# The exact pieces of the normalised tokens of a second attention, in two tiles, one for each half of the tokens

## The chip, the cores and the metric

The kernel runs on one core of a Trainium2 chip. Its time is the time of one execution on the device in microseconds (us); shown is the median of three runs. TensorE (PE) multiplies matrices, VectorE (DVE), ScalarE (ACT) and GpSimd (POOL) work on elements, and SyncE (SP) starts transfers (DMA).

## The reference

1024 tokens of 512 channels pass through four blocks with a residual sum each: attention A (32 heads of 16 channels in 8 groups), a mixture of 8 experts of rank 16 on top of a base layer, attention B (32 heads of 128 channels, 8 groups of keys and values, weights of 4 bits with a scale for each 128 input channels, rotary positions, causal), and the same mixture of experts again.

```python
def _dequant_matmul(x, qw, scales):
    w = (qw.astype(jnp.float32) - ZERO) * jnp.repeat(scales, GS, axis=0)
    return x @ w
...
x = x + _L0_attn_a_ref(_layernorm(x, axis=-1), ...)
x = x + _L0_ffn_ref(_layernorm(x, axis=-1), ...)
x = x + _L0_attn_b_ref(_layernorm(x, axis=-1), ...)   # q, k, v and output by _dequant_matmul
x = x + _L0_ffn_ref(_layernorm(x, axis=-1), ...)
```

## The kernel before

The tokens stay on the chip in x_sb, in four blocks `a` of 256 tokens (two halves of 128 rows each). The sequence is attention A (to about 480 us), the first experts (to about 550), attention B head by head (to about 1380), and the second experts.

For attention B the normalised tokens are kept turned (channels on the 128 partitions) and in two pieces that sum to the number exactly: a high one in the format that TensorE takes at full rate, and a low one with the rest. Both lie in one tile, x_hl, of 128 partitions x 2 pieces x 4 chunks of channels x 1024 tokens. They are made by `halves_of_x(a, xn)`, once for each block: `norm.turned` transposes the eight 128x128 squares of the block on TensorE (line 185) into two PSUM banks, two chunks in each; for each bank ScalarE copies the high piece (line 755) and VectorE subtracts it for the low piece (line 756). The rows `xn` come from `ready(a)`: statistics (lines 149 and 150 on VectorE), root on ScalarE (154), reciprocal and shift on VectorE (155, 156), and then the rows by VectorE (162) and ScalarE (170). The statistics of a block need its sum with the experts' output (line 670, VectorE).

They are read by `scaled`, which makes one half (512 tokens) of a head's query, key or value: for each of four chunks `exact` multiplies the whole-number weights with the high piece (line 798) and the low piece (799) into one PSUM bank, and the result is scaled and summed, the first chunk by ScalarE (line 810), the others by VectorE (812). PSUM has five banks (`ac_ps`) for all of this. Queries and keys are then rotated: a transfer through SyncE's queue (822, 823) swaps halves of the partitions and lines 824 to 826 multiply and add, on GpSimd, for the first query on VectorE.

The order of TensorE's instructions is the order of the program text (`tc.manual_schedule`). Around the change it is: halves_of_x of blocks 0 and 1 between parts of the experts; keys(0) and queries(0) on the first half of the tokens; the last experts' matmuls; halves_of_x(2); values(0) on the first half (the matmuls of all four chunks); halves_of_x(3); then the first head's scores with the second halves of keys(0) and queries(0), woven in by two lists of due work (`short`, `long`). The order on VectorE, ScalarE, GpSimd and SyncE is made when the kernel is built, by a planner that takes the program's order as priority and its own estimate of times. The same library adds all waits between engines, from what each instruction reads and writes of a tile.

In the last head `reload(i, total)` brings the experts' weights back from DRAM in seven parts into the room of x_hl (lines 1087 and 1088); the second experts read them there.

Of the kernel before, what the change touches and what calls it, by code (L numbers as in the profile page):

```python
# [11 lines left out]
F32 = mybir.dt.float32  # L12
F32R = mybir.dt.float32r
# [3 lines left out]
ALU = mybir.AluOpType  # L17
# [3 lines left out]
P = 128  # L21
S = 1024
C = 512
NC_ = C // P
# [17 lines left out]
def kernel(  # L42
# [28 lines left out]
    nc = tc.nc  # L71

    def pool(stack, name, bufs=1, space=None):
        kw = {} if space is None else {"space": space}
        return stack.enter_context(tc.tile_pool(name=name, bufs=bufs, **kw))
# [28 lines left out]
    order = const.tile([P, 1, E], F32, name="order")  # L104
# [10 lines left out]
    def place_ffn_weights(room):  # L115
        at = 0
        for name, n, width in ("base", NC_, C), ("ar", NC_, AR), ("b", 1, C), ("bias", 1, C):
            fw[name] = room[:, at : at + n * width].rearrange("p (c o) -> p c o", o=width)
            at += n * width
        return room[:, :at]  # L120
# [17 lines left out]
    class Norm:  # L138
# [13 lines left out]
        def scale(self, a0, a1):  # L152
            some = slice(2 * a0, 2 * a1)
            nc.scalar.activation(self.rstd[:, some], self.mv[:, some, 1], AF.Sqrt, bias=eps_t)
            nc.vector.reciprocal(self.rstd[:, some], self.rstd[:, some])
            nc.vector.scalar_tensor_tensor(
                self.shift[:, some], self.mv[:, some, 0], -1.0, self.rstd[:, some], ALU.mult, ALU.mult
            )
# [16 lines left out]
                scale=self.rstd[:, t + 1 : t + 2],  # L175
            )

        def turned(self, a, xn, bank, natural, store):

            for cp in range(NC_ // 2):  # L180
                tp = bank()
                by = tp.rearrange("q (c h p) -> q c h p", c=2, h=2)
                for c in range(2):
                    for h in range(2):
                        nc.tensor.transpose(by[:, c, h, :], xn[:, h, ts(2 * cp + c, P)], ident)  # L185
                order = "q c (p h) -> q c h p" if natural else "q c (h p) -> q c h p"
                store(
                    lambda dst: dst[:, 2 * cp : 2 * cp + 2, ts(a, 2 * P)].rearrange(order, h=2), by
                )

    def to_xT(place, tp):
# [2 lines left out]
    norm = Norm()  # L194
# [478 lines left out]
    def attention_b():  # L673
# [5 lines left out]
        with ExitStack() as ph:  # L679
            one = pool(ph, "b_one")  # L680
# [2 lines left out]
            ac_ps = pool(ph, "b_ac_ps", 5, PSUM)  # L683

            v_sb = one.tile([P, NT, G * DB], F32, name="v_sb")
            x_hl = one.tile([P, 2, NC_, S], F32R, name="x_hl")
            cos_sb = one.tile([P, S], F32, name="cos_sb")
            sin_sb = one.tile([P, S], F32, name="sin_sb")
            yT = shared.rearrange("p (c s) -> p c s", c=NC_)
# [61 lines left out]

            def halves_of_x(a, xn):
                def store(place, tp):
                    high = place(x_hl[:, 0])
                    nc.scalar.copy(high, tp)
                    nc.vector.tensor_tensor(place(x_hl[:, 1]), tp, high.bitcast(F32), ALU.subtract)  # L756

                norm.turned(a, xn, bank, True, store)

# [35 lines left out]
            def exact(ps, lhsT, high, low):  # L797
                nc.tensor.matmul(ps, lhsT, high, start=True, stop=False)  # L798
                nc.tensor.matmul(ps, lhsT, low, start=False, stop=True)  # L799
# [2 lines left out]

            def scaled(acc, w, scale, half):

                tok = ts(half, C)
                for c in range(NC_):
                    pp = ac_ps.tile([P, C], F32, tag="acc", name="pp")
                    exact(pp, w[:, c], x_hl[:, 0, c, tok], x_hl[:, 1, c, tok])
                    if c == 0:
                        nc.scalar.activation(acc, pp, AF.Copy, scale=scale(c))  # L810
                    else:
                        nc.vector.scalar_tensor_tensor(acc, pp, scale(c), acc, ALU.mult, ALU.add)  # L812
                    yield 2 * FAST

            def rotated(dst, w, scale, engines=(nc.gpsimd, nc.gpsimd)):

                for half, eng in enumerate(engines):
                    tok = ts(half, C)
                    acc = work.tile([P, C], F32, tag="acc", name="acc")
                    yield from scaled(acc, w, scale, half)  # L820
                    turned = work.tile([P, C], F32, tag="turned", name="turned")
                    nc.sync.dma_start(turned[0:64], acc[64:128])
                    nc.sync.dma_start(turned[64:128], acc[0:64])
                    eng.tensor_tensor(dst[:, tok], acc, cos_sb[:, tok], ALU.mult)  # L824
                    eng.tensor_tensor(turned, turned, sin_sb[:, tok], ALU.mult)
                    eng.tensor_tensor(dst[:, tok], dst[:, tok], turned, ALU.add)  # L826
                    yield 0
# [10 lines left out]
            def values(g):  # L838

                vT = one.tile([P, S], F32, tag="vT", name=f"vT_{g}")  # L840
                w = wvs.pop(g)
                for half in range(2):
                    acc = work.tile([P, C], F32, tag="acc", name="acc")
                    yield from scaled(acc, w, lambda c: v_sc[:, c, g : g + 1], half)

                    nc.scalar.copy(
                        vT[:, ts(half, C)].rearrange("d (k r j) -> d k j r", j=4, r=32),
                        acc.rearrange("d (k j r) -> d k j r", j=4, r=32),
                    )
                    yield 0  # L850
                waiting.append([len(issued) + 2, [("v", g), 4 * FAST, turned_values(g, vT)]])
# [9 lines left out]
            def probabilities(n, t):  # L861

                qT, kT = qTs[n], kTs[n // J]
                keys = (t + 1) * P
                wide = t >= NT // 2 or (n == 0 and t == 1)
                sc = sc_ps.tile([P, S if wide else C], F32, tag=f"sc{wide}", name="sc")
                for k0 in range(0, keys, C):
                    k1 = min(k0 + C, keys)
                    nc.tensor.matmul(sc[:, k0:k1], qT[:, ts(t, P)], kT[:, k0:k1], start=True, stop=True)  # L869
                at = len(issued) - NT * (HEADS - 1)  # L870
                slot = LAST[at] if at >= 0 else SLOTS[len(issued) % 3]
                p = x_sb[:, slot].rearrange("p h c -> p (h c)")
                issued.append(t)
                p = p[:, :keys]

                m = work.tile([P, 1], F32, tag="m", name="m", bufs=3)
                nc.vector.tensor_tensor_reduce(  # L877
                    p, sc[:, :keys], causal[:, S - keys :], -1.0, BIG, ALU.add, ALU.min, m
                )
                total = work.tile([P, 1], F32, tag="total", name="total", bufs=3)  # L880
                nc.scalar.activation(p, p, AF.Exp, bias=m, scale=-1.0, accum_out=total)  # L881
                return p, total
# [5 lines left out]
            flat = xT.rearrange("p c o -> p (c o)")  # L888

            def placed(n, t, p):  # L890
# [37 lines left out]
            place = {  # L928
                0: flat[:, :384],
                2: flat[:, 384:1792],  # L930
                3: flat[:, 1792:3712],
                1: one.tile([P, 896], F32, name="pT_1"),
            }
            place = {k: v.rearrange("p (i x) -> p i x", i=4) for k, v in place.items()}
# [68 lines left out]
            with tc.manual_schedule(engines={mybir.EngineType.PE}):  # L1003
                with ExitStack() as fs:
# [34 lines left out]
                    moe.base(4)  # L1039
                    moe.finish(3)  # L1040
                    halves_of_x(0, xns[0])
                    ready(1)
                    moe.base(5)
                    moe.finish(4)
                    moe.base(6)
                    moe.finish(5)
                    halves_of_x(1, xns[1])
                    ready(2)
                    short += [[("k", 0), 16 * FAST, keys(0)], [("q", 0), 16 * FAST, queries(0)]]
# [5 lines left out]
                    moe.finish(7)  # L1055
                    ready(3)
                    halves_of_x(2, xns[0])
                    short.append([("v", 0), 16 * FAST, values(0)])
                    for _ in range(4):
# [20 lines left out]

                def reload(i, total):

                    flat = x_hl.rearrange("p i c s -> p (i c s)")
                    room = place_ffn_weights(flat.bitcast(F32))
                    width = -(-room.shape[1] // (NT - 1))
                    part = slice(i * width, min((i + 1) * width, room.shape[1]))
                    nc.vector.tensor_copy(flat[:, part.start : part.start + 1], total)
                    nc.sync.dma_start(room[:, part], w_kept[:, part])
# [9 lines left out]
                for n in range(HEADS):  # L1098
# [16 lines left out]
                    for i, t in enumerate(TURNS if n else [0, 1, 2, 4, 3, 5, 6, 7]):  # L1115
# [5 lines left out]
                        p, total = probabilities(n, t)  # L1121
# [163 lines left out]
```

## Time and profile before

| | us |
|---|---|
| median of three runs | 1445.62 (1443.53 to 1448.45) |
| the profiled execution | 1443.47 |
| its span, first to last instruction | 1441.6 |
| TensorE busy in the span | 1387.7 (96%) |
| VectorE, ScalarE, GpSimd busy | 1188.9, 868.2, 596.9 |
| lines 798 and 799 reading x_hl, 384 matmuls each | 183.5 and 153.0 |

| stretch, us | TensorE busy | VectorE busy | ScalarE busy | TensorE clock granted |
|---|---|---|---|---|
| 500 to 530 | 29.21 | 14.42 | 6.86 | 1.00 |
| 530 to 550 | 16.77 | 15.88 | 7.77 | 0.83 |
| 550 to 600 | 44.60 | 39.77 | 29.82 | 0.93 |
| 600 to 1300 | 690.30 | 629.35 | 474.40 | 1.00 |

Busy times are of one profiled execution. Matmuls overlap in their pipeline, so a busy TensorE is not one at its peak. An idle time in the timeline is put down to what ended it; a wait for several things is put down to the last.

### The profile page before, as it was taken

What the parts mean: (1) busy time and instruction counts of PE and PEld (TensorE: products, weight loads), DVE (VectorE), ACT (ScalarE), POOL (GpSimd) and SP (SyncE); (2) the same over time, 40 slices, a digit from 0 to 9 for tenths busy, and PEclk for the clock granted to TensorE, in tenths of its full rate; (3) what the DMA queues carried; (4) which work ended last, traced back from release to release, by engine and by line L of the source; (5) the groups of instructions that cost most, each with busy time, mean ns of one, the idle gap of its engine ahead of it and who ended that gap; (6) DMA issues with size and microseconds to landing.
All of it is one profiled execution on the core that took longest, in us unless ns stands there. A gap on an engine that the chain in (4) does not pass through costs nothing. (4 is left out here: it accounts for less than half of the span.)

```text
span 1441.6 us, 21145 instructions
## 1 busy us (share of the span) xinstructions
PE 1387.7 (96%) x6711; PEld 882.1 (61%) x6711; DVE 1188.9 (82%) x2491; ACT 868.2 (60%) x1642; POOL 596.9 (41%) x505
## 2 busy tenths in 40 slices
PE   6999999999999998899999999999999999999888
PEld 4444444444444545677677777777777777777664
DVE  4799979979893658789898998999998998989774
ACT  2166757757677325676576676676666676666630
POOL 4200000000000616566666767657667566645230
PEclk9999999999999998999999999999999999999999
DMA  4352423324240213655566565655655655565711
GB/s 126 61 100 48 69 42 56 62 35 70 48 134 2 86 66 98 153 138 148 140 147 156 126 149 145 149 143 140 149 140 145 145 137 141 139 137 119 193 57 59
DMA packets 113183, 158.47 MB, mean 110 GB/s; under 512 B 35008, under 2 KB 86912, under 8 KB 112944
## 3 DMA queue, kind: packets, MB, share of 16 engines
q1 hardware_dynamic: 106252, 135.51, 40.3%
q0 software_dynamic: 6752, 21.57, 5.6%
q8 instruction: 54, 0.88, 0.2%
q14 instruction: 57, 0.47, 0.1%
q10 hardware_dynamic: 68, 0.03, 0.0%
HBM read 33.03 MB, written 6.05 MB: 27 GB/s over the span
## 5 line engine op out<-in xcount | busy, mean ns | idle before, releaser
L387 ACT ACTIVATE pT<-st 128x512 f32<-128x512 f32 x512 | 264.6, 603 | 128.7 <-PE st L383 109.6
L343 DVE TENSOR_REDUCE m<-sc 128x1 f32<-128x512 f32 x512 | 319.8, 682 | 25.8 <-PE st L375 19.8
L869 PE MATMUL sc<-kT,qT 128*128 128x512 f32 (+3 forms) x768 | 292.0, 489 | 2.4 <-POOL qT L826 1.3
L881 ACT ACTIVATE x_sb<-x_sb,m 128x768 f32<-128x768 f32 (+7 forms) x256 | 197.0, 769 | 120.4 <-DVE m L877 117.7
L949 PE MATMUL pc<-xT,v_sb 128*128 128x256 f32 (+1 forms) x1024 | 240.4, 361 | 14.2 <-DMA xT<-blocks 14.0
L886 ACT ACTIVATE x_sb<-x_sb,total 128x768 f32<-128x768 f32 (+7 forms) x256 | 195.5, 771 | 70.4 <-DVE total L885 69.0
L949 PEld LDWEIGHTS pc<-xT,v_sb 128*128 128x128 f32 x1024 | 190.7, 189 | 49.5 <-issue 17.2
L877 DVE CUSTOM_DVE_ANT_0 x_sb<-sc,causal 128x768 f32<-128x768 f32 (+7 forms) x256 | 191.4, 748 | 27.5 <-PE sc L869 26.1
L334 PE MATMUL sc<-ks,qs 64*128 64x512 f32 x512 | 186.7, 448 | 5.4 <-DVE m L343 2.6
L798 PE MATMUL pp<-x_hl,w 128*128 128x512 f32 x384 | 183.5, 478 | 2.2 <-ACT acc L810 1.6
L869 PEld LDWEIGHTS sc<-kT,qT 128*128 128x128 f32 x768 | 139.0, 192 | 74.5 <-issue 61.7
L383 PE MATMUL st<-ms_q,ones 64*128 64x512 f32 x512 | 178.0, 413 | 0.8 <-DMA ms_q<-mT 0.7
L375 PE MATMUL st<-qs,ks 64*128 64x512 f32 x512 | 176.0, 423 | 1.4
L334 PEld LDWEIGHTS sc<-ks,qs 64*128 64x128 f32 x512 | 83.9, 184 | 146.3 <-DVE m L343 129.6
L900 DVE STREAM_TRANSPOSE blocks<-x_sb 128x640 f32<-128x640 f32 (+3 forms) x128 | 133.2, 1041 | 27.1 <-ACT x_sb L886 21.2
L799 PE MATMUL pp<-x_hl,w 128*128 128x512 f32 x384 | 153.0, 399 | 2.2 <-DVE x_hl L756 2.2
L127 POOL DMA_DIRECT2D shared<-in_b_base_dram x1 | 0.5, 547 | 367.3 <-DVE m L343 367.3
L812 DVE SCALAR_TENSOR_TENSOR acc<-pp,q_sc,acc 128x512 f32<-128x512 f32 x192 | 140.7, 733 | 10.4 <-ACT acc L810 7.4
L706 POOL TENSOR_SCALAR w<-r 128x512 fp32r<-128x512 int32 x80 | 119.5, 1493 | 71.0 <-PE pp L799 47.0
L408 PE MATMUL po<-pT,v_sb 128*32 128x512 f32 x1024 | 136.6, 605 | 0.0
L824 POOL TENSOR_TENSOR qT<-acc,cos_sb 128x512 f32<-128x512 f32 x62 | 80.1, 1292 | 131.9 <-DVE acc L812 120.8
L798 PE MATMUL py<-ctx,w 128*128 128x512 f32 x256 | 133.0, 520 | 1.2 <-DVE xT L136 0.7
(178 smaller groups left out, 2196.8 us busy)
## 6 DMA issues: line engine op xcount, KB each, us to landing
xT<-blocks SPq DMA_DIRECT2D x128, 240.0 KB, 4.4
xT<-blocks SPq DMA_DIRECT2D x128, 176.0 KB, 3.4
turned<-acc SPq DMA_DIRECT2D x160, 128.0 KB, 3.1
pT<-x_sb SPq DMA_DIRECT2D x128, 112.0 KB, 3.6
qs<-q_hl SPq DMA_DIRECT2D x128, 64.0 KB, 2.4
qs<-shared SPq DMA_DIRECT2D x128, 64.0 KB, 2.6
r<-in_qwq_dram POOLq DMA_DIRECT2D x32, 256.0 KB, 3.6
r<-in_qwo_dram POOLq DMA_DIRECT2D x32, 256.0 KB, 3.6
```

The source lines that it names most:

```text
L334: nc.tensor.matmul(sc, qs[pair % NS][rows, jj, ts(t, P)], ks[pair // 2 % NS][rows, ts(half, C)], start=True, stop=True,)
L343: nc.vector.tensor_reduce(ms[pair][:, at : at + 1], sc, AX.X, ALU.max, negate=True)
L375: nc.tensor.matmul(st, ks[pair // 2 % NS][rows, ts(kt, P)], qs[pair % NS][rows, u // 2, ts(u % 2, C)], start=True, stop=False,)
L383: nc.tensor.matmul(st, ones[rows], ms_q[pair % 2][rows, u // 2, ts(u % 2, C)], start=False, stop=True)
L387: nc.scalar.activation(pTs[pair, kt][:, u], st, AF.Exp, scale=DA**-0.5)
L798: nc.tensor.matmul(ps, lhsT, high, start=True, stop=False)
L799: nc.tensor.matmul(ps, lhsT, low, start=False, stop=True)
L869: nc.tensor.matmul(sc[:, k0:k1], qT[:, ts(t, P)], kT[:, k0:k1], start=True, stop=True)
L877: nc.vector.tensor_tensor_reduce(p, sc[:, :keys], causal[:, S - keys :], -1.0, BIG, ALU.add, ALU.min, m)
L881: nc.scalar.activation(p, p, AF.Exp, bias=m, scale=-1.0, accum_out=total)
L886: nc.scalar.activation(p, p, AF.Copy, scale=total)
L949: nc.tensor.matmul(pc[:, 2 * P * i + lo : 2 * P * (i + 1)], v_sb[:, k, ts(g, DB)], some, start=(k == 0), stop=(k == 2 * pair + 1),)
```

## The change

x_hl becomes a list of two tiles, x_hl0 for tokens 0 to 511 and x_hl1 for tokens 512 to 1023, each of 128 x 2 x 4 x 512, which together have the size of the old one. `halves_of_x(a)` writes into tile a // 2, at block a % 2 of it (the new argument `at` of `turned`); `scaled` reads the tile of its half; `reload` uses the first tile.

```diff
-        def turned(self, a, xn, bank, natural, store):
+        def turned(self, a, xn, bank, natural, store, at=None):
...
-                    lambda dst: dst[:, 2 * cp : 2 * cp + 2, ts(a, 2 * P)].rearrange(order, h=2), by
+                    lambda dst: dst[:, 2 * cp : 2 * cp + 2, ts(a if at is None else at, 2 * P)].rearrange(
+                        order, h=2
+                    ),
+                    by,
...
-            x_hl = one.tile([P, 2, NC_, S], F32R, name="x_hl")
+            x_hl = [one.tile([P, 2, NC_, C], F32R, name=f"x_hl{h}") for h in range(2)]
...
-                    high = place(x_hl[:, 0])
+                    hl = x_hl[a // 2]
+                    high = place(hl[:, 0])
                     nc.scalar.copy(high, tp)
-                    nc.vector.tensor_tensor(place(x_hl[:, 1]), tp, high.bitcast(F32), ALU.subtract)
-
-                norm.turned(a, xn, bank, True, store)
+                    nc.vector.tensor_tensor(place(hl[:, 1]), tp, high.bitcast(F32), ALU.subtract)
+
+                norm.turned(a, xn, bank, True, store, a % 2)
...
-                tok = ts(half, C)
+                hl = x_hl[half]
                 for c in range(NC_):
                     pp = ac_ps.tile([P, C], F32, tag="acc", name="pp")
-                    exact(pp, w[:, c], x_hl[:, 0, c, tok], x_hl[:, 1, c, tok])
+                    exact(pp, w[:, c], hl[:, 0, c], hl[:, 1, c])
...
-                    flat = x_hl.rearrange("p i c s -> p (i c s)")
+                    flat = x_hl[0].rearrange("p i c s -> p (i c s)")
```

## The prediction

> **What bounds the kernel now.** I read the page first, for where TensorE is not full.
>
> ```profile
> PE 1387.7 (96%) x6711; PEld 882.1 (61%) x6711; DVE 1188.9 (82%) x2491; ACT 868.2 (60%) x1642; POOL 596.9 (41%) x505
> PE   6999999999999998899999999999999999999888
> PEclk9999999999999998999999999999999999999999
> ```
>
> TensorE is busy 96% of the span. Apart from the ends, its one thin place is slices 16 and 17 (about 540 to 610 us), where its clock dips as well: there the first mixture of experts hands over to the second attention, and there the normalised tokens are split into their pieces. Next, the list of waits for 530 to 560 us.
>
> ```profile
> PEld pp L799 <- DVE x_hl L756: 2.7, 2, 2.5
> PE pp L799 <- DVE x_hl L756: 2.2, 1, 2.2
> ```
>
> Line 799 (the matmul with the low piece) waited for line 756 (VectorE writing a low piece) once for 2.2 us. The timeline of TensorE shows which one (columns: start, duration, engine, line, operation; in brackets the idle time before and what ended it):
>
> ```profile
> 539.90 0.40 PE L799 MATMUL pp<-x_hl,w 128*128 128x512 f32 x1
> 540.14 0.48 PE L798 MATMUL pp<-x_hl,w 128*128 128x512 f32 x1
> 542.81 0.80 PE L799 MATMUL pp<-x_hl,w 128*128 128x512 f32 x1 [2.19 <-DVE x_hl L756]
> ...
> 544.68 0.63 PE L799 MATMUL pp<-x_hl,w 128*128 128x512 f32 x1
> 546.01 2.11 PE L185 MATMUL bank<-ident,xn 128*128 128x128 f32 x8 [0.70 <-DVE xn L162]
> ```
>
> These are values(0) on the first half of the tokens, run between the transposes of token blocks 2 and 3. The waiting matmul reads the low piece of channel chunk 1, tokens 0 to 511. The write that it waits for is of block 2: chunks 0 and 1, tokens 512 to 767. They share no element. But in one tile of 1024 tokens a chunk the write spans offsets 512 to 1791, and the read, 1024 to 1535, lies inside; the read of chunk 0 (0 to 511) lies outside, and its matmul at 539.90 did not wait. So I read it as a false dependency on address ranges. The matmuls of keys(0) and queries(0) just before read blocks 0 and 1, which they need; those after 546 us on the second half need all that they wait for; later nothing writes the tile until the reload at 1348 us.
>
> The timeline of VectorE over the same time:
>
> ```profile
> 542.02 0.16 DVE L150 BATCH_NORM_AGGREGATE mv<-st 128x2 f32<-128x6 f32 x1
> 542.10 0.65 DVE L756 TENSOR_TENSOR x_hl<-bank,x_hl 128x512 fp32r<-128x512 f32 x1
> ...
> 543.94 0.15 DVE L155 RECIPROCAL rstd<-rstd 128x2 f32<-128x2 f32 x1
> 544.01 0.73 DVE L812 SCALAR_TENSOR_TENSOR acc<-pp,v_sc,acc 128x512 f32<-128x512 f32 x1
> ...
> 545.33 0.54 DVE L162 TENSOR_SCALAR xn<-x_sb,mv,rstd 128x512 f32<-128x512 f32 x1
> 545.78 1.60 DVE L812 SCALAR_TENSOR_TENSOR acc<-pp,v_sc,acc 128x512 f32<-128x512 f32 x2
> ```
>
> Each instruction starts as the one before it ends: VectorE is full from 538.81 to 547.38. Its line 162 makes the rows of block 3, for which the transposes at 546.01 wait, and it is late because VectorE is full, not because TensorE was.
>
> **The change, part by part.** No instruction is added or removed: the eight writes by ScalarE (0.63 us each), the eight by VectorE (0.68) and all matmuls keep their sizes, and two tiles take the room of one. No DMA moves to another queue.
>
> The wait of 2.19 us goes. The five value matmuls behind it would follow the one at 540.14 at the warm spacing of 0.23 us (549.57 to 549.80): the first at about 540.38, the last done at 540.38 + 4 x 0.23 + 0.40 = 541.70, in place of 544.68 + 0.63 = 545.31. That is 3.6 us earlier for them. If the last chunk has to wait for a PSUM bank that the first line 756 frees at 542.75, they are done by about 543.6, which is still ahead of what comes.
>
> What is late next is the rows of block 3. The transposes behind the values on TensorE's queue need line 162 (done at 545.87) and ScalarE's line 170 (546.31). Neither needs a value matmul, so both stay, and so does 546.01. TensorE's idle time before it grows from 0.70 to 546.01 - 541.70 = 4.31 us, and the sum on the path is 0. What lies behind (keys(0), queries(0) on the second half, the first head) starts where it did. Three additions for the values leave VectorE's queue earlier at best, but vT, which they feed, is not transposed before 577.92.
>
> The clock: granted over the stretches that the page's dip covers it reads
>
> ```profile
> 530.00:542.50 12.50, 10.29 (x37) 5.56 (x35) 9.51 (x18) 4.20 (x7) 4.16 (x3) 1.00 0.30 89
> 542.50:549.40 6.90, 5.89 (x18) 4.37 (x19) 6.05 (x13) 2.97 (x5) 0.00 (x0) 0.51 0.11 45
> ```
>
> (the 1.00 and 0.51 after the five engines are the clock). In stretches of 1 us it is 0.76 for 542 to 543 and 0.82 for 549 to 550, so half clock lasts from 542.5 to 549.4; a second such time runs from 559.6 to 566.4. Both last 6.8 us, and the edges lie 3.4 us or a multiple apart, so I take it that the clock is decided in periods of 3.4 us: 539.1 to 542.5 held the idle time and brought half clock. After the change that period is nearly full and the next, 542.5 to 545.9, is empty: half clock from 545.9, and back at 549.4, since the work from 546.0 to 549.4 is the same. The five values run warm, the rest as now: again 0. Bounds: from -1.9 us (the clock stays full; the eight transposes cost 1.04 in place of 2.11, and four matmuls spare 0.2 each) to +3.0 (half clock lasts one period more; about 15 matmuls between 549.4 and 552.8 at 0.43 in place of 0.23). I take 0, the reading nearest to this row.
>
> A rule of the Trainium skill speaks against the change here: "TensorE: Matmul & The Clock Gate", the table in "Why this matters for your kernels", wants no idle gaps of over some 3 us, since one idle window halves the clock. By it the present 2.19 us should be harmless and the new 4.31 us would bring a half clock that was not there, an estimated 1.9 us by the prices above. The trace disagrees on the first half: 2.19 us was enough, so half clock is in the time of before already.
>
> The reload in the last head goes to the first tile: 4 x 512 + 4 x 136 + 512 + 512 = 3616 words of 4096, in the same seven transfers, from 1348.6 us, after the last read of the tokens (1329.5): 0.
>
> One cost no row shows. Only TensorE's order is written out; VectorE, ScalarE, GpSimd and SyncE take theirs from a planner that goes by its own estimate of when things are ready, and without the wait it sees the values ready earlier. On the spot, the two additions that now stand behind line 162 could be put ahead of it: +1.5 us (545.78 to 547.38, less overlap). Or the rows could move ahead of the queries' lines 825, 826 and the first addition: line 162 from 545.33 to about 543.57 (after the second line 756 and a reciprocal), -1.8. Beyond the spot the order of all 32 heads may differ. I bound that by the busy time of TensorE in stretches of 100 us:
>
> ```profile
> 600.00:700.00 100.00, 97.72 (x409) 72.98 (x409) 86.89 (x189) 69.73 (x131) 65.45 (x54) 1.00 0.57 146
> 800.00:900.00 100.00, 99.35 (x420) 74.57 (x418) 90.93 (x194) 67.91 (x127) 69.14 (x57) 1.00 0.60 147
> sum 700.00, PE 690.30 PEld 517.13 DVE 629.35 ACT 474.40 POOL 466.27; mean PE 98.61 PEld 73.88 DVE 89.91 ACT 67.77 POOL 66.61
> ```
>
> Idle are 9.7 us in seven stretches; all like the worst (2.28) would be 16.0, +6.3; all like the best (0.65) 4.6, -5.1. I take 0: the two plans meet again at the rows of block 3.
>
> The sum is 0 on the profiled execution of 1443.47 us (a span of 1441.6 and 1.87 around it). The median of the runs is 2.15 above that, so I forecast 1445.6.
>
> **The rivals.** *The wait is not false, or is a bank's.* Then nothing changes, 1445.6 too. Against it: the waiting low matmul adds to the bank that its high one at 540.14 had already, and it starts 0.06 us after line 756 ends.
>
> *Slower: the value additions pass the rows of block 3.* All of VectorE's time up to 545.9 is taken, so each that gets ahead of line 162 delays the transposes. Two cost 1.5 us, transposes at 547.5, and the period 545.9 to 549.4 is then half empty, so the slow clock lasts one more: +3.0. Together +4.5, or 1450.1. It decides from two additions on; one is absorbed by the margin of the period. For it: additions that are ready early are what fills a queue while line 155 waits for ScalarE's square root. Against it: lines 756 and 825 are there to fill that place, and are so now. A worse order in the heads adds up to 6.3 instead.
>
> *Faster: the rows come forward, or a better order in the heads.* Rows 1.8 us earlier, and with the shorter gap the clock perhaps kept, 1.9: -3.7, or 1441.9; that alone ends within the bound for no change, and the heads like their best stretch, -5.1 or 1440.5, end beyond it. For it: 8.6 us of idle TensorE between 530 and 600 us (3.23 and 5.40) can shrink. Against it: nothing in the change puts the rows first.
>
> **How the numbers follow.** No change, 0.40; its own range is 1443.1 to 1448.1, the 0 to 1.5 of the spot and the some 2.5 by which runs of one kernel stray (1443.53 to 1448.45). Slower rival 0.33 and faster 0.27, both mostly by the orders in the heads: those of four queues for 890 us are unknown, and the spot offers a push later that fits greedy filling. About 0.3%, 4.3 us, is what a measurement of this kernel can tell from no change. The range goes from 1445.6 - 5.1 - 2 = 1438.5 to 1445.6 + 6.3 + 1.5 = 1453.4.
>
> **What would show it.** Right: no wait of line 799 for line 756 between the transposes of blocks 2 and 3, the values done near 541.7, then some 4 us until line 185 follows line 162 at the same 546.0, half clock until 549.4, the heads unchanged. The slower rival shows value additions (L812, v_sc) ahead of line 162; the faster one line 162 near 543.6. Wrong altogether: the 2.19 us still there, or a different busy share of TensorE between 600 and 1300 us with this spot as I said.

## The result, and the profile after

The changed kernel takes 1448.66 us (median of 20 runs, 1445.68 to 1451.40) beside 1445.95 us for the kernel before (20 runs, 1441.79 to 1449.46). The ratio is 1.0019, with a 95% interval of 1.0011 to 1.0027: some 2.7 us slower. That is less than the 0.3% I had named as what can be told from no change, but with twenty runs on each side it can be told. The profiled execution took 1448.36 us, with a span of 1446.5.

Lines behind the edits have moved: 705 and 706 of before are 708 and 709 of after, and 755, 756, 798, 799, 810, 812, 824, 846, 877, 881, 885 and 900 are 759, 760, 802, 803, 814, 816, 828, 850, 881, 885, 889 and 904.

The page of after, its span, busy times, and the rows of TensorE and of its clock:

```profile
span 1446.5 us, 21140 instructions
PE 1388.6 (96%) x6711; PEld 881.8 (61%) x6711; DVE 1191.5 (82%) x2491; ACT 868.5 (60%) x1642; POOL 596.9 (41%) x505
PE   6999999999999997899999999999999999999888
PEclk9999999999999998999999999999999999999999
```

The same instructions, TensorE busy 0.9 us longer, VectorE 2.6 and the others within 0.3, and the same thin place in the row. First the spot of the prediction, in the timeline of TensorE:

```profile
540.59 0.40 PE L803 MATMUL pp<-x_hl,w 128*128 128x512 f32 x1
545.08 2.11 PE L185 MATMUL bank<-ident,xn 128*128 128x128 f32 x8 [4.09 <-DVE xn L162]
```

The wait of 2.19 us for line 756 is gone; the last value matmul ends at 540.99, and the transposes of block 3 then wait 4.09 us for line 162. In VectorE's timeline that line stands as it did, behind one value addition and ahead of two:

```profile
543.09 0.72 DVE L816 SCALAR_TENSOR_TENSOR acc<-pp,v_sc,acc 128x512 f32<-128x512 f32 x1
...
544.40 0.53 DVE L162 TENSOR_SCALAR xn<-x_sb,mv,rstd 128x512 f32<-128x512 f32 x1
544.86 1.59 DVE L816 SCALAR_TENSOR_TENSOR acc<-pp,v_sc,acc 128x512 f32<-128x512 f32 x2
```

545.33 had become 544.40. But this whole execution was 0.93 us ahead of the profiled one of before already at 530 us, ahead of the changed place (start of the fourth low piece: 529.91 before). With that taken off, the rows and the transposes stand exactly where they stood. From here on I call "lag" what an execution is behind the one of before, with its own difference at 530 us taken off.

The lag is 0 at line 162, +1.29 at the second causal mask (line 877 on VectorE, eight for each head), and +3.77 at the ninth, the first of the second head (579.72 us before). The heads behind that are as they were: the windows of after (columns as in the prediction) give for 600 to 1300 us

```profile
600.00:700.00 100.00, 97.69 (x403) 72.40 (x401) 85.22 (x186) 69.58 (x131) 64.80 (x55) 0.98 0.59 145
...
sum 700.00, PE 691.08 PEld 516.58 DVE 628.37 ACT 474.15 POOL 466.97; mean PE 98.73 PEld 73.80 DVE 89.77 ACT 67.74 POOL 66.71
```

691.08 us of TensorE beside 690.30. TensorE was less busy in between:

```profile
550.00:600.00 50.00, 41.46 (x156) 27.30 (x155) 40.32 (x76) 26.67 (x49) 33.37 (x27) 0.96 0.45 110
```

41.46 us where before had 44.60. So I compared the order of instructions in the two built kernels, engine by engine. TensorE's and SyncE's are the same. ScalarE's, VectorE's and GpSimd's differ in one stretch only, from just behind line 162 to about 576 us; all of heads 1 to 31 is the same. The beginnings of the three, in line numbers of before (k, q, v: of the key, query, value; 881 with its table load):

```diff
 ScalarE, from the last pieces of the tokens
-755 755 846vT 810k 881 810q 886 881 810q 886 881 810q
+755 846vT 755 881 810k 810q 886 881 886 881 810q 886 810q
 VectorE, behind line 162
-812v 812v 756 756 877 812k 812k 812k 885 812q 900 812q 812q 877 824q
+812v 812v 756 877 756 885 812k 812q 812k 812q 812k 812q 877 824q
 GpSimd: 706 unpacks weights, 705 requests the next 256 KB of them
-706 705 824k 706 705 825k 826k
+706 705 706 705 824k 825k 826k
```

In the trace, ScalarE first, before:

```profile
548.16 0.63 ACT L755 CAST x_hl<-bank 128x512 fp32r<-128x512 f32 x1 [0.23 <-PE bank L185]
548.67 1.14 ACT L846 COPY vT<-acc 128x512 f32<-128x512 f32 x1
549.61 0.67 ACT L810 ACTIVATE acc<-pp,k_sc 128x512 f32<-128x512 f32 x1
550.30 1.28 ACT L881 ACT_TABLE_LOAD   x1
```

and after:

```profile
546.88 1.15 ACT L850 COPY vT<-acc 128x512 f32<-128x512 f32 x1
547.81 0.68 ACT L759 CAST x_hl<-bank 128x512 fp32r<-128x512 f32 x1
548.50 1.28 ACT L885 ACT_TABLE_LOAD   x1
...
550.20 0.67 ACT L814 ACTIVATE acc<-pp,k_sc 128x512 f32<-128x512 f32 x1
```

The copy of the values went ahead of the last high piece, and the table load with the first exponential ahead of the first scaling of the key. On VectorE the key's three additions stood in a row before,

```profile
550.31 2.46 DVE L812 SCALAR_TENSOR_TENSOR acc<-pp,k_sc,acc 128x512 f32<-128x512 f32 x3 [0.59 <-ACT acc L810]
...
555.46 0.69 DVE L824 TENSOR_TENSOR qT<-acc,cos_sb 128x512 f32<-128x512 f32 x1
```

and after they take turns with the query's:

```profile
550.90 0.75 DVE L816 SCALAR_TENSOR_TENSOR acc<-pp,k_sc,acc 128x512 f32<-128x512 f32 x1 [0.41 <-PE pp L803]
552.16 0.75 DVE L816 SCALAR_TENSOR_TENSOR acc<-pp,q_sc,acc 128x512 f32<-128x512 f32 x1 [0.51 <-ACT acc L814]
...
554.14 0.74 DVE L816 SCALAR_TENSOR_TENSOR acc<-pp,k_sc,acc 128x512 f32<-128x512 f32 x1
...
555.82 2.24 DVE L828 TENSOR_TENSOR qT<-acc,cos_sb 128x512 f32<-128x512 f32 x1
```

The key is done at 554.88 in place of 552.77, a lag of 3.04. GpSimd's timeline before:

```profile
553.57 1.30 POOL L824 TENSOR_TENSOR kT<-acc,cos_sb 128x512 f32<-128x512 f32 x1
554.96 1.49 POOL L706 TENSOR_SCALAR w<-r 128x512 fp32r<-128x512 int32 x1
556.74 0.80 POOL L705 DMA_DIRECT2D r<-in_qwq_dram  x1 [0.29 <-POOL w L706]
```

and after:

```profile
553.63 1.48 POOL L709 TENSOR_SCALAR w<-r 128x512 fp32r<-128x512 int32 x1
555.41 0.80 POOL L708 DMA_DIRECT2D r<-in_qwq_dram  x1 [0.29 <-POOL w L709]
556.23 1.28 POOL L828 TENSOR_TENSOR kT<-acc,cos_sb 128x512 f32<-128x512 f32 x1
```

The request of 256 KB now starts 0.45 us behind the transfer that swaps the halves of the key (issued at 554.96). By its releaser, the next query's first scaling on ScalarE waits for that transfer (it writes a buffer that the transfer still reads); it empties a PSUM bank, and TensorE waits for the bank. ScalarE's timeline before:

```profile
557.52 0.69 ACT L810 ACTIVATE acc<-pp,q_sc 128x512 f32<-128x512 f32 x1 [1.33 <-DMA turned<-acc]
```

and TensorE behind it:

```profile
558.26 0.51 PE L798 MATMUL pp<-x_hl,w 128*128 128x512 f32 x1 [1.62 <-ACT acc L810]
```

ScalarE's after:

```profile
559.99 0.69 ACT L814 ACTIVATE acc<-pp,q_sc 128x512 f32<-128x512 f32 x1 [0.45 <-DMA turned<-acc]
```

and TensorE's:

```profile
560.73 0.79 PE L802 MATMUL pp<-x_hl,w 128*128 128x512 f32 x1 [3.73 <-ACT acc L814]
```

The scaling lags by 559.99 - 557.52 + 0.93 = 3.40 us. TensorE's wait, 1.62 before, is now 3.73.

### The profile page after: what moved, and what is told of

It is laid out like the page before. It is cut to its first block, busy times and chain, and to the rows that moved or that the text cites. A ratio compares the mean times of both kernels' runs of the same rounds, so it can differ in the third digit from the quotient of the medians.

```text
span 1446.5 us, 21140 instructions
## 1 busy us (share of the span) xinstructions
PE 1388.6 (96%) x6711; PEld 881.8 (61%) x6711; DVE 1191.5 (82%) x2491; ACT 868.5 (60%) x1642; POOL 596.9 (41%) x505
```

## The experiments

Theory "order": two tiles cost nothing by themselves; the planner, seeing the values ready earlier, puts three engines into another order behind the rows, and that order is slower. Rival "idle": the 4.1 us of idle TensorE in one piece are what costs, by the clock. Rival "clock or chance later": the lag comes from half-clock periods that fall elsewhere.

All twelve kernels make their order with the same edit. An edge between two instructions of one engine fixes which is issued first and adds no wait. The table lists names of instructions; I give the orders below in line numbers of before.

```diff
+ORDER = {"ACT": [...], "DVE": [...], "POOL": [...]}
...
+    for names in ORDER.values():
+        for one, two in zip(names, names[1:]):
+            tc.add_manual_dep(made[two], one, in_order, reason="order")
```

Each was timed in turns with the kernel before, and the ratios are taken from that: two_old, one_new, old_act and rows_first on one chip, dve_early, dve_late, pool_new and rows_first2 on another, the other four on a third. Their line numbers are 8 further on than those of after (one_new: than those of before). What is said of places (lags, waits) comes from one profiled execution of each.

Executions of one kernel differ in the clock that TensorE is granted on the mean, and in time with it. Before was timed 103 times beside the experiments, at 0.989 to 0.998 (mean 0.9930): the 28 executions at 0.991 or less have a median of 1447.86 us, the 46 at 0.994 or more 1443.80. A straight line through all 103 gives some 1.1 us for each 0.001. By it I estimate what each kernel takes over before at one clock:

| kernel | mean clock | over before at one clock, us |
|---|---|---|
| after | 0.9933 | 3.2 +- 0.5 |
| two_old | 0.9935 | -0.2 +- 1.0 |
| one_new | 0.9922 | 3.1 +- 0.8 |
| old_act | 0.9921 | 3.6 +- 0.7 |
| dve_early, dve_late | 0.9940, 0.9932 | 2.2 +- 0.5, 1.8 +- 0.9 |
| pool_new | 0.9939 | 2.1 +- 0.7 |
| early_pool | 0.9931 | 2.1 +- 0.7 |
| old_pool, late_request | 0.9943, 0.9936 | 2.4 +- 1.1, 1.4 +- 0.7 |
| rows_first, 2, 3 | 0.9947, 0.9941, 0.9944 | -0.1 +- 0.6, -0.1 +- 1.0, 0.4 +- 0.9 |

The clock is given to three places, and an order may itself move it, so these are estimates beside the ratios and not in their place.

### The two halves of the change apart

two_old has the two tiles, with the order of before on the three engines (the lines with a minus above).

> Two tiles, with ScalarE, VectorE and GpSimd held to the order that they have in the kernel before (by edges that fix only the order of issue; all that differs from the changed kernel lies between the rows of block 3 and the end of the first head). Theory 'order' (the 2.7 us are lost by the planner's new order after the rows of block 3, and the two tiles alone cost nothing): the time of before, 1446.0 less 0 to 0.5 us; the value matmuls end early as in the changed kernel, then TensorE is idle for some 4 us, and the first mask of the first head stands where it does before. Theory 'idle' (the values done early leave TensorE idle for 4.1 us in one piece, half clock falls on more of the next matmuls, and the order is innocent): slower by about 2.7 us, as the changed kernel, 1448.7.

Ratio 0.9995 (0.9982 to 1.0008), lag at the ninth mask -0.24. Its TensorE:

```profile
541.03 0.40 PE L811 MATMUL pp<-x_hl,w 128*128 128x512 f32 x1
545.52 2.11 PE L193 MATMUL bank<-ident,xn 128*128 128x128 f32 x8 [4.09 <-DVE xn L170]
```

The idle time is 4.09 us in one piece, as in after, and it costs nothing that shows. "Idle" falls.

one_new has one tile, with the order of after (the lines with a plus).

> One tile as before, with ScalarE, VectorE and GpSimd held to the order of the changed kernel. Theory 'order': slower by about 2.7 us, 1448.7, although the wait of 2.19 us for the low piece is still there; in its profile the first heads are some 4 to 5 us late from the third mask on. Theory 'idle': the time of before, 1446.0.

Ratio 1.0029 (1.0017 to 1.0041), lag +4.08. The wait for the low piece is in it still:

```profile
543.42 0.50 PE L807 MATMUL pp<-x_hl,w 128*128 128x512 f32 x1 [2.32 <-DVE x_hl L764]
```

The order makes it slower without the two tiles; the two tiles without the order do not. This settles between the first two theories. At one clock the two stand at -0.2 and 3.1 us, and after, at the clock of before, at 3.2: so the third theory, that the clock differs, does not carry the loss either.

### Which engine's order

old_act: after, with ScalarE's order put back.

> Two tiles, ScalarE alone held to the order of before; VectorE and GpSimd keep the changed kernel's order. Theory 'order', if ScalarE's part of it (the copy for vT ahead of the last high piece, and the exponential with its table ahead of the first scaling of the keys) carries the loss: 0 to 1 us over before. If VectorE's part carries it (additions for keys and queries in turns, the product of the query with the cosine beside GpSimd's): still 2 to 3 us over. Theory 'idle': 2.7 over.

Ratio 1.0031 (1.0018 to 1.0044), lag +5.01. ScalarE, whose lines look the worst in the comparison, does not carry the loss.

dve_early: two_old with VectorE's new order as far as the last of the six additions, so key and query in turns.

> Two tiles, ScalarE and GpSimd in the order of before; VectorE takes the first part of its new order alone (the first mask ahead of the last low piece, and the additions for keys and queries of the second half in turns, in place of the keys' three first), and from the second mask on that of before. If this part carries the loss (the key is finished some 2 us later, and with it the swap by transfer, the buffer for the next query and GpSimd's product, which then falls on VectorE's own): 2 to 5 us over before, 1448 to 1451. If the loss is in the later part of the order: within 1 us of before.

Ratio 1.0006 (0.9995 to 1.0016), lag +1.44.

dve_late: two_old with VectorE's new order from behind the first query's product and the mask that follows it.

> The opposite: VectorE in the order of before up to the additions for keys and queries of the second half, in the new order from the second mask on (transposes and reciprocals earlier, rotation of the query later). If the early part carries the loss: within 1 us of before, 1445 to 1447. If the late part does: 2 to 5 us over.

Ratio 1.0006 (0.9993 to 1.0020), lag +1.06, then +3.45 at the 33rd mask, with a half-clock period at 606.8 between.

pool_new: two_old with GpSimd's new order.

> Two tiles, ScalarE and VectorE in the order of before, GpSimd alone in its new order (unpacking of weights and a request ahead of the key's product with the cosine). If GpSimd's order matters by itself, the second half of the key is later by the 1.5 us of an unpacking and the kernel 1 to 2 us over before; if it only follows the others: within 0.7 us of before.

Ratio 1.0003 (0.9992 to 1.0015), lag +0.12.

By ratio none of the three parts that were tried alone can be told from before (ScalarE's new order and VectorE's whole one were not tried alone). At one clock each of the three stands some 2 us over. Two that go together, then:

early_pool: the new orders of dve_early and pool_new in one kernel.

> Two tiles in the order of before, with the first part of VectorE's new order and GpSimd's new order (each alone cost under 1 us). Theory 'together': 3 to 4 us over before, 1449 to 1450, with the wait of 3.5 us or more of TensorE near 557 us. If the parts only add: 0.9 to 1.5 us over.

Ratio 1.0019 (1.0006 to 1.0032), the ratio of the change itself, TensorE's wait 3.62 us, and a lag of +3.38, where the parts alone had 1.44 and 0.12. In time the three intervals overlap, and at one clock early_pool (2.1) stands where its parts stand (2.2 and 2.1). That the parts don't add is therefore seen in the lags of single executions and not shown in time. ScalarE's timeline in dve_early:

```profile
558.22 0.69 ACT L822 ACTIVATE acc<-pp,q_sc 128x512 f32<-128x512 f32 x1 [1.14 <-DMA turned<-acc]
```

and in early_pool:

```profile
560.18 0.69 ACT L822 ACTIVATE acc<-pp,q_sc 128x512 f32<-128x512 f32 x1 [3.18 <-DMA turned<-acc]
```

GpSimd's request of 256 KB in dve_early, where the key's transfer is issued at 555.31:

```profile
558.81 0.80 POOL L716 DMA_DIRECT2D r<-in_qwq_dram  x1 [0.29 <-POOL w L717]
```

and in early_pool, where that transfer is issued at 555.24:

```profile
555.63 0.79 POOL L716 DMA_DIRECT2D r<-in_qwq_dram  x1 [0.29 <-POOL w L717]
```

The table follows the lags (us; the key's end is counted from the start of line 162; the third column is the time from there to the next query's first scaling, the fourth the lag of that scaling by the sum of the two):

| kernel | key done | to the scaling | scaling's lag | lag at 580 |
|---|---|---|---|---|
| before | 7.44 | 4.75 | 0 | 0 |
| pool_new | 7.42 | 4.57 | -0.20 | +0.12 |
| dve_early | 10.67 | 2.98 | +1.46 | +1.44 |
| early_pool | 10.79 | 5.01 | +3.61 | +3.38 |
| after | 10.48 | 5.11 | +3.40 | +3.77 |

Before, the key's swap ran beside a request too: the one at 552.75 for value weights (swap issued at 552.85). A key that is 3.2 us late is mostly clear of that one (in dve_early, requested at 553.12), the time to the scaling is 1.8 us less, and half of the lateness is won back. GpSimd's new order puts the next request just there and takes the gain away; with a key in time it adds no lag, since a request runs beside the swap anyway (there the scaling, at 557.07, waited for GpSimd's product of the key). The second half-clock time begins behind the scaling in all five and lasts 6.8 us in before, pool_new and early_pool, 3.4 in dve_early and after, so the last column has the clock in it too.

### Taking one cost out of the changed kernel

old_pool: after, with GpSimd's order put back.

> The changed kernel, with GpSimd alone put back to the order of before. Theory 'together' (neither VectorE's nor GpSimd's new order costs much alone; together they make the key late by 2 us, let a request of weights run beside the swap that the late key waits for, and put GpSimd's product of the key on VectorE's product of the query): most of the loss goes, 0 to 1 us over before, 1446 to 1447; VectorE's product of the query with the cosine takes 0.7 to 0.9 us in place of 2.24, and TensorE's wait at 557 us falls from 3.7 to some 1.6. If ScalarE's and VectorE's orders carry the loss together without GpSimd: 2 to 3 us over.

Ratio 1.0011 (0.9997 to 1.0026), lag +1.37; key to scaling 3.40, TensorE's wait 1.97 in place of 3.73, VectorE's product 0.97 us. The wait falls much as 'together' had it, but the time, 1.6 us over before (0.4 under to 3.8 over), lies between the two forecasts and decides nothing.

late_request: after, with the one request moved behind the key's rotation on GpSimd (706 705 706 824k 825k 826k 705).

> The changed kernel, with one instruction moved: GpSimd's request of the next query's weights (256 KB) is issued behind the key's product, rotation and sum in place of ahead of them. If the request beside the swap is what makes TensorE wait at 557 us: the swap's buffer is free some 2 us earlier (3 us after the key is done in place of 5) and the kernel 0.5 to 1.5 us over before. If it is the key's lateness and the collision of the two products alone: still 2 to 3 us over.

Ratio 1.0012 (1.0000 to 1.0025), lag +2.70; key to scaling 3.53, TensorE's wait 2.12. The scaling is 1.59 us better than in after, yet only 1.07 of it is left at 580 us. That can be the weights, which come later, or the clock: half clock lasts from 560.4 to 567.3 here, from 560.7 to 564.1 in after. No run separates the two. In both runs the scaling starts as ScalarE is through with the work before it (559.78 and 558.18, no idle time), so with the request moved the swap is no longer what it waits for. Their intervals in time overlap that of after, so that time is saved by it is not shown; 1.0012 lies between the two forecasts.

### A better order

The prediction's faster rival had the rows of block 3 first. rows_first: two tiles, the old order, and VectorE's stretch ahead of the transposes rearranged.

```diff
-670 824q 149 149 150 756 150 756 825 155 812v 826 156 162 812v 812v 756 756
+670 149 149 150 150 824q 155 156 162 756 756 825 812v 826 756 812v 756 812v
```

> Two tiles, the order of before, and VectorE besides makes the rows of block 3 ahead of the low pieces of block 2, the rotation of the first query and the additions for the values. The rows should be ready some 2.5 to 3 us earlier. Theory 'order' with the rows as what is late (the prediction's reading): TensorE's idle time before the transposes of block 3 falls from 4 to about 1.5 us and the kernel is 2 to 4 us faster than before, 1442 to 1444. If something after that (the swap of the query by transfer, the exponential's table) sets the first head's pace: within 1 us of before.

Ratio 0.9988 (0.9977 to 0.9999), lag -0.55: the one kernel here that is faster than before, and with it than after, by more than its interval, though by little: some 1.7 us. The expectation was 2 to 4. Its executions also had the highest mean clock, 0.9947 beside 0.9930, and at one clock nothing of the gain is left (-0.1 +- 0.6). Whether the order raised the clock or had luck with it, no run separates; that the order itself is faster is not shown. Its TensorE:

```profile
543.05 1.25 PE L193 MATMUL bank<-ident,xn 128*128 128x128 f32 x8 [1.80 <-DVE x_hl L768]
545.59 0.77 PE L881 MATMUL sc<-kT,qT 128*128 128x128 f32 x2 [1.29 <-DVE qT L838]
```

Its ScalarE:

```profile
548.00 1.13 ACT L858 COPY vT<-acc 128x512 f32<-128x512 f32 x1 [3.04 <-DVE acc L824]
548.93 0.66 ACT L822 ACTIVATE acc<-pp,k_sc 128x512 f32<-128x512 f32 x1
```

The transposes come 2.3 us earlier (546.01 less this run's 0.68 is 545.33), though the rows are ready 2.8 us earlier: they now wait for a low piece of block 2 (line 768 there). Two more waits eat the rest: the first scores now wait for the query's rotation (1.29), and ScalarE stands 3.04 us in front of the values' copy, for which the additions are not done, with the key's scaling queued behind it at the old time.

rows_first2 takes both waits out: the query's rotation ahead of the value additions, and the key's scaling (810k) ahead of the values' copy (846).

> As the kernel with the rows of block 3 first on VectorE, and besides the first query's rotation ahead of the additions for the values (TensorE waited 1.29 us for it in that kernel's profile), and ScalarE scales the keys of the second half ahead of the copy for vT (it stood idle 3.04 us for that). The start of the first head should move 1 to 2 us further ahead: 2 to 4 us faster than before, 1442 to 1444. If the gain is again gone by the second mask (as there, where the first mask was 1.6 us and the second 0.7 us ahead): 1 to 2 us faster.

Ratio 0.9989 (0.9974 to 1.0003), lag -2.89. Its first scaling of the next query is 1.3 us ahead of before; the rest of the 2.89 may be the clock's, as half clock ends at 549.6 in this execution and does not come back before 580. In time it can't be told from rows_first.

rows_first3 adds both of GpSimd's requests behind the key's rotation, to clear the swap.

> As the second kernel with the rows of block 3 first, and both of GpSimd's requests of weights moved behind the key's product, rotation and sum, so that none runs beside the swap of the key. The next query's first scaling should follow the key by 3 us in place of 4.7. If transfers set this spot: 3 to 5 us faster than before, 1441 to 1443. If the products and VectorE's queue set it: as that kernel, 1 to 3 us faster.

Ratio 0.9990 (0.9976 to 1.0004), lag +0.73. The swap was not what the scaling waited for any more: the key is done at 550.90 and the scaling starts at 555.23, 4.33 us later, as ScalarE is through with the exponential before it (554.73 + 0.51 = 555.24), which waited 2.57 us for VectorE's mask. The expectation missed that.

## Why the prediction was wrong, and where it was right

**The wait.** Right. It was a false dependency on ranges of addresses: with two tiles it is gone, the values are done at 540.99 (541.9 with the 0.93 put back; 541.70 forecast).

**What is late next.** Right: line 162 at the same relative time, 4.09 us of idle time in place of 4.31, and nothing gained. two_old prices this part alone at 0.9995.

**The clock.** 0 was right as a size, by two_old. The placing was not: half clock lasted from 543.6 to 550.4 in after, two periods and not the one from 545.9 that I had worked out, and from 545.1 to 548.5 in two_old. Windows of after over this stretch:

```profile
530.00:543.60 13.60, 10.66 (x40) 5.96 (x38) 10.88 (x21) 4.28 (x8) 4.18 (x3) 1.00 0.27 80
543.60:550.40 6.80, 5.32 (x17) 4.38 (x18) 4.45 (x11) 4.81 (x8) 0.00 (x0) 0.50 0.00 0
```

Where the periods fall differs from one execution to the next, so I should not have carried their edges over from one trace to another. The second half-clock time is shorter in after (560.7 to 564.1) and another has come at 608.5; the total up to 1300 us is 13.6 us in both. Over its twenty executions after had a mean clock of 0.9933, before 0.9930 over 103. So it is not the clock that makes after slower.

**The order.** Here the forecast failed, in the sentence "I take 0: the two plans meet again at the rows of block 3." They met there, to the instruction, and parted directly behind. I had given the order two places: the spot, up to the rows (+1.5 to -1.8), and the heads (+6.3 to -5.1). It acted in neither, but in the 30 us between, where the second halves of key and query are woven into the first scores. The term I sized at 0 measures +3.4 us at the scaling, +3.8 at 580 us, and 2.7 in time (1.6 to 3.9); one_new, which has the order without the two tiles, prices it at 4.2 (2.5 to 5.9). The heads did as forecast, 691.08 us of TensorE beside 690.30, and so none of the signs that I had named for being wrong came up. My own range for no change was also summed too short: 1.5 of the spot and 2.5 of straying reach 1449.6, not 1448.1.

What should have warned me: the trace of before has TensorE waiting 1.62 us at 558.26 for ScalarE, for a swap, for the key. That chain has little slack: of the 3.2 us by which dve_early's key is late, 1.46 arrive at the scaling. I had priced a value that is ready 3.6 us earlier by who waits for it (vT, not before 577.92) and not by what its copy (line 846) can now overtake on ScalarE, or its additions' place on VectorE.

**The slower rival** had the right sign and cause, the planner's order, at the wrong place: no value addition passed line 162. **The faster rival's** first half was tried: transposes 2.3 us earlier came with 1.7 us, not the 3.7 of rows and clock, and the 1.7 may be the clock's alone.

**What stays open.** Which part of the new order carries the loss in time: the lags point at the late key with the request beside its swap, but at one clock every part that was tried costs some 2 us. That the planner takes another order because the values are ready earlier is argued from its inputs, not shown. VectorE's late order (dve_late) has a lag of its own of about 1 us that I did not take apart. After old_act the lag at 580 us (+5.01) is 2 us over that of its scaling (+3.01), and I have not followed it. Single executions of one order differ by 2 to 3 us behind 640 us (two_old, with the order of before, has a lag of +0.39 at the 65th mask and +2.67 at the 129th, at a ratio of 0.9995), so lags that far on are not used.

## What to carry to other kernels

Where a planner or compiler orders some of the engines, a removed wait is also a changed input to it: compare the order of the instructions on every engine first, before reading a single time, and hold the old order once to price the edit alone. Cut a false dependency only with a look at what it had kept apart; here its removal was worth 0, and with the new order that came of it the kernel took 0.19% more. Lags on one chain need not add (1.44 and 0.12 apart, 3.38 together): follow the chain (key, swap, buffer, bank) through each experiment. And where a gain is as small as 0.1%, set the granted clock of the executions beside their times before crediting the edit.

## What the hardware showed

**Two products at once.** A VectorE product of this shape with two inputs in SBUF takes 0.68 us while GpSimd is idle (lines 825 and 826 of before, at 543.34 and 544.66). The product of the query takes 0.81 to 2.40 where GpSimd has a product under way or starting. In nine traces (after, one_new, old_act, dve_early, pool_new, old_pool, early_pool, late_request, rows_first3) it ends 0.54 to 0.57 us after GpSimd's product ends, whatever its own start: in after GpSimd ends at 556.23 + 1.28 = 557.51 and VectorE at 555.82 + 2.24 = 558.06. That looks like waiting out GpSimd's instruction and then running. The Trainium skill, "SBUF — State Buffer", section "Who interferes with whom", gives the rule: a VectorE instruction with two SBUF inputs contends with a GpSimd instruction that reads SBUF, over a port pair that is an exclusive lock. These nine agree. Two things don't fit: VectorE started 0.41 us ahead of GpSimd's product in after and still was the one to wait (GpSimd's request was under way then, 555.41 to 556.21), and in before the same product ran in 0.69 us, from 555.46 to 556.15, in the midst of GpSimd's unpack, which reads SBUF (554.96 to 556.45, undisturbed as well). The same shows in two_old, dve_late, rows_first and rows_first2. By pool_new (2.40 us for the product, lag +0.12) the collision leaves no lag at 580 us.

**The clock.** From 530 us on, every half-clock time in these traces is 3.4 or 6.8 us, but for the last of each, which the end cuts off. The Trainium skill, "TensorE: Matmul & The Clock Gate", section "Part 1: The HAM clock gate", has windows of 3413 ns that run freely; that agrees, and the free running is what my forecast of their edges left out. Its limit of some 3 us for a gap, which the prediction cites, decides nothing here: in before half clock followed idle times of 2.19 us (542.5) and 1.62 us (559.6), and 4.09 us in two_old cost no time that shows.
